# Two graph layers on 32 batches: place tables stored as rows, h scatters two steps apart, and the second regrouped batch's gathered tiles loaded later

## The chip, the core and the metric

The kernel runs on one core of a Trainium2 chip. The metric is the device time in microseconds (us) of one execution; lower is better. Before the change the median of three runs is 1025.54 us (1025.52 to 1026.99). The profile comes from one further execution, taken with the hardware profiler on.

## The reference

There are 32 batches of 512 nodes with 512 features. Two layers follow each other, each with a residual:

```python
h = jnp.maximum(_layernorm(x), 0.0)
x = x + (einsum('nm,bmd->bnd', adj, h) @ weight + bias)      # layer 0: graph aggregation
h = jnp.maximum(_layernorm(x), 0.0)
x = x + attention(h, adj)                                    # layer 1
# attention: 8 heads, scores + (1 - adj) * -1e9, softmax, @ v, @ Wo + bo
```

The adjacency matrix `adj` is sparse with weights between 0.05 and 1 (and ones on the diagonal, before scaling). In layer 1 the mask term is `(1 - adj) * -1e9`: a key whose weight is the largest of its row wins the softmax by a margin that no score can close. So the attention of a row is the value of a single node, the row's strongest neighbour.

## The kernel before, in words

**What is computed.** The kernel checks at run time that each row has a clear strongest neighbour; then layer 1 is a gather: `h` of the chosen rows goes through one combined matrix `wvo` (value times output projection), giving `z`, and each node adds the `z` row of its neighbour. Only rows that are somebody's strongest neighbour ("used", at most 336 of 512) need a `z`. Everything is float32, and the large products of 512x512 are done with a seven-product scheme (`product`, line 502): pieces "p1" to "c21", eight matmuls each.

**Two phases.** Batches 0 to 3 (`FIRST` = 4) run in a first phase with dense aggregation. Meanwhile the class `Plan` (line 974) works out a new order of the nodes, in which the adjacency matrix falls into blocks. A flag decides at a branch (lines 927 to 936), and the second phase, `sparse`, aggregates with fewer matmuls (`spread`, line 609). Batches up to 4 are held in natural order (`natural(b)`, line 458), later ones in the new order ("regrouped"). A regrouped batch's `x` rows are gathered from memory by `load_x`, and three extra 128-row tiles `plan.gx` (called `at` in the profile) by `load_g`; these are normalised into `plan.HG` (called `adjT`) before `spread`.

**The order of the work is written out by hand.** For every `b` there is a list of 21 steps (`todo`). `put(batch, step, f)` hangs a function on a step. Steps 0 to 6 go with the seven pieces of layer 0 of batch b, steps 7 to 13 with the aggregation of batch b+1 (in the sparse phase its four pieces take steps 7+8, 9+10, 11+12 and 13), steps 14 to 20 with the seven pieces of layer 1 of batch b-1. Each step's functions are issued after the matmuls of that piece and before the instruction that takes its result from PSUM. Each engine works through its own queue in this order. DMAs that POOL issues additionally wait for the last such result to be taken (`behind`, line 466).

**Round trips through memory around the change.**

- `put_h` (line 648) stores `h` of layer 1. For a natural batch it is four indirect scatters on POOL (line 661), one per 128 rows, to the places in `dest`, each followed by a small memset. For a regrouped batch it is four plain DMAs on SP (line 657).
- `get_h` (line 669) reads the used rows back with four DMAs on SP (line 672), after all four scatters of that batch have landed. `transpose_h` (line 723, VectorE) takes them in the next batch's steps 5, 7 and 8 (later in batch 1).
- `put_z` (line 734) stores `z` with DMAs on SP (line 741); `finish` (line 746) adds the `z` rows to `X` with four accumulating gathers on POOL (line 473); `store` writes the result.

**Place tables.** Three tables of 512 integers are written to memory and looked up with gathers of single elements:

- `table` from `dest` (`places`, line 579), made in batch 1 step 0 and looked up in steps 3 to 6;
- `posd` from `posi` (`save_pos`, line 1242), in batch 2 step 9, looked up in batch 5 (`look_1`);
- `tab2` from `pi` (`save_pi`, line 1248), in batch 6 step 4, looked up later in batch 6 (`look_2`).

In all three the source tile has node c*128+p in partition p, column c, and one DMA on SP stores it with the pattern "(c p) o -> p (c o)".

**Normalisation of the gathered tiles.** For batch 5 an object `lead` (`NormAct`: the statistics by ScalarE with accumulating activations, line 394, into a scrap tile) handles `gx` at the start of batch 4. For batch 6 and later a `NormMore` object (line 940) does it: `more_stats` (line 954) at steps 13 to 18 of the batch before the one that uses it, `more_relu` (line 967) at steps 1 to 3.

Of the kernel before, what the change touches and what calls it, by code (L numbers as in the profile page):

```python
# [8 lines left out]
F32 = mybir.dt.float32  # L9
I32 = mybir.dt.int32  # L10
# [8 lines left out]
P = 128  # L19
# [389 lines left out]
def single_path(ctx: ExitStack, tc: tile.TileContext, x, adj, out, kept, room):  # L409
    nc = tc.nc  # L410
    B, N, D = x.shape
# [10 lines left out]
    dram = ctx.enter_context(tc.tile_pool(name="dram", bufs=1, space=DRAM))  # L422
    dest = consts.tile([P, C], I32, name="dest")
    place = consts.tile([P, C], I32, name="place")
    pos = consts.tile([P, C], F32, name="pos")
# [29 lines left out]
    def run_phase(batches, sparse, small, ps_m, ps_t):  # L455
# [109 lines left out]
        def number_rows():  # L565
            counts = ps_t.tile([P, DC, P], F32, name="pt")
            nc.tensor.matmul(counts[:, 1, 0:C], upper, used, start=True, stop=True)
            nc.tensor.matmul(counts[:, 2, 0:1], upper, ones[:, 0:1], start=True, stop=True)
            nc.vector.tensor_add(pos, counts[:, 1, 0:C], before[:, 0:C])
            for m in range(C):  # L570
                nc.vector.tensor_scalar(other[:, m:m + 1], counts[:, 2, 0:1], float(m * P), before[:, C:C + 1],
                                        op0=ALU.add, op1=ALU.add)
            nc.vector.tensor_sub(other, other, pos)
            nc.vector.tensor_sub(pos, pos, other)
            nc.vector.tensor_mul(pos, pos, used)
            nc.vector.tensor_add(pos, pos, other)
            nc.vector.tensor_copy(dest, pos)

        def places():
            table = dram.tile([N, 1], I32, name="table", bufs=1)  # L580
            nc.sync.dma_start(table.rearrange("(c p) o -> p (c o)", p=P), dest)
            return table
# [93 lines left out]

        def get_all(b):
            for c in range(C):
                gather(hs[0][:, c, :], hs_d[b % 3], idx[:, c, 0:1] if natural(b) else plan.pq[:, c:c + 1])
# [69 lines left out]

        def fetch(b):  # L750
            for c in range(C):
                gather(late_z[b][:, c, :], z_d[b % 3], place_of(b, c))
# [22 lines left out]
        for b in batches:  # L775
            todo = [[] for _ in range(21)]

            def put(batch, step, f, *args):
                if 0 <= batch < B:
                    todo[step].append(lambda: f(batch, *args))  # L780

            if sparse and b == FIRST:
                for j in range(3):
                    put(b + 1, 1 + j, lambda b, j: lead.stats(j), j)
                put(b + 1, 3, lambda b: lead.power())
                put(b + 1, 4, lambda b: lead.offset())
                for j in range(3):
                    put(b + 1, 4 + (j + 1) // 2, lambda b, j: lead.relu(j), j)
            if sparse:
                for j, step in enumerate((6, 7, 8) if b == FIRST else (4, 5, 6)):  # L790
                    put(b + 2, step, load_g, [j])
                if last:
                    put(b + 1, 0, lambda b, n=last[-1]: n.offset())
                    for c in range(4):
                        put(b + 1, c, lambda b, c, n=last[-1]: n.relu(c), c)
                    for c in range(3):
                        put(b + 1, 1 + c, lambda b, c, n=last[-1]: n.more_relu(c), c)
# [5 lines left out]
            if b == B - 1:  # L803
                put(b - 2, 15, fetch)
            elif b < B:
                for c, step in enumerate((9, 11, 13, 15) if sparse and b == FIRST else (7, 9, 11, 13) if sparse else
                                         (4, 5, 6, 7) if ordered and b == FIRST - 1 else (1, 2, 3, 4)):
                    put(b - 2, step, finish, [c])
            elif not sparse:
                put(b - 2, 1, fetch)  # L810
# [30 lines left out]
            put(b, 10, lambda b: halves[0].relu(1, b < B - 1))  # L841
            put(b, 10, put_h, [0, 1] if sparse or b == B - 1 else [0])
            put(b, 11, lambda b: halves[1].relu(0, b < B - 1))
            if b < B - 1 and not sparse:
                put(b, 11, put_h, [1])
            put(b, 12, lambda b: halves[1].relu(1, b < B - 1))
            put(b, 12, put_h, [2, 3] if sparse or b == B - 1 else [2])
            if b < B - 1 and not sparse:
                put(b, 13, put_h, [3])
            if b < B - 1:  # L850
                if natural(b - 2):
                    put(b - 2, 19 if sparse and b == FIRST else 14 if sparse else 12, store)
                else:
                    for c in range(C):
                        put(b - 2, 14 + 2 * c, store, [c])
            if b < B - 1:
                put(b, 17, get_h)
            else:
# [10 lines left out]
            ahead = []  # L869
            kind = NormAct if on_act else NormMore if sparse else Norm  # L870
            if b == 0:
                put(2, 1, lambda b: ahead.append(ln0(b, kind)))
                for c, step in enumerate((1, 1, 2, 2)):
                    put(2, step, lambda b, c: ahead[0].stats(c), c)
            else:
                put(b + 2, 4 if sparse else 8, lambda b: ahead.append(ln0(b, kind)))
                for c, step in enumerate((9, 10, 13, 13)):
                    put(b + 2, step, lambda b, c: ahead[0].stats(c), c)
                if sparse:
                    put(b + 2, 4, lambda b: ahead[0].more(plan.gx, plan.HG, 3))  # L880
# [10 lines left out]
            if b == 0:  # L891
                put(0, 1, lambda b: number_rows())
                for i in (2, 3):
                    put(0, 8, lambda b, i: sum_b(nc, w0_t, w0_s, i), i)
                    put(0, 9, lambda b, i: sum_a(nc, wvo_t, wvo, i), i)
# [78 lines left out]
class Plan:  # L974
    def __init__(self, tc, consts, dram, adj, kept, upper, B):
# [5 lines left out]
        def t(name, shape, dt=F32):  # L981
            return consts.tile([P] + shape, dt, name=name)
# [22 lines left out]
        self.valid, self.gn, self.qn = t("valid", [3]), t("gn", [3]), t("qn", [C])  # L1005
        self.posi = t("posi", [C], I32)
        self.off = t("boff", [B, C])
        self.xi, self.gi = t("xi", [B, C], I32), t("gi", [B, 3], I32)
        self.pi, self.pq, self.place, self.pqf = t("pi", [C], I32), t("pq", [C], I32), t("pplace", [C], I32), t("pqf", [C])
        self.flag = consts.tile([1, 1], I32, name="flag2")  # L1010
# [242 lines left out]

    def packed(self):
        v = self.nc.vector
        v.tensor_copy(self.pqf, self.pq)
        v.tensor_copy(self.rank, self.pq)
# [3 lines left out]
        v.tensor_copy(self.place, self.pqf)  # L1261

# [22 lines left out]
    def schedule(self):  # L1285
        def at(b, step, f, *args):
            self.steps.setdefault(b, []).append((step, lambda ps_t, behind: f(*args)))
# [53 lines left out]
        at(7, 5, self.packed)  # L1341

# [260 lines left out]
```

## Time and profile before

| What | Value |
|---|---|
| median of 3 runs | 1025.54 us |
| profiled execution, its own time | 1038.36 us |
| span of the profiled execution | 1036.5 us |
| TensorE (PE) busy | 997.9 us, 96% |
| VectorE (DVE) busy | 800.1 us, 77% |
| ScalarE (ACT) busy | 585.8 us, 57% |
| GpSimd (POOL) busy | 589.1 us, 57% |
| DMA packets under 512 B | 17873 of 161140 |
| layer 0 of batches 3, 4 and 5 begins at | 153.25, 190.80, 229.16 us |

How to read it: all times count from the start of the span, in us. The slices are fortieths of the span (25.9 us each), a digit is the busy share in tenths. PEclk is the TensorE clock that was granted. A line of the wait view reads: engine, what waited, what ended the wait, and then the total in us, the number of waits and the longest. A line of the window view reads: stretch, its length, the busy time of PE, PEld (weight loads), DVE, ACT and POOL with their instruction counts, the granted clock, the mean busy share of the DMA engines (overlapping packets can bring it above 1) and the GB/s moved. A line of the timeline reads: start, duration, engine, line, operation, what is written from what, and in brackets the idle time before it and what ended it. "issue" means that no releaser is seen.

### The profile page before, as it was taken

How to read it: one execution, taken by the hardware profiler on the slowest of the kernel's cores; microseconds unless marked ns; L12 is line 12 of the kernel's file. 1: busy time of each engine (PE TensorE's matmuls, PEld its weight loads, DVE VectorE, ACT ScalarE, POOL GpSimd, SP SyncE). 2: the span in 40 equal slices, each digit the busy share in tenths (PEclk: the TensorE clock that was granted, in tenths of full speed). 3: DMA queues.
4: the chain of work that ended last, by engine and by line, in shares of the span. 5: the costliest groups of instructions: out<-in, count | busy, mean ns of one | idle time of the engine just before them, and what ended most of it. 6: DMA issues, size and time to landing. Idle time of an engine off the chain costs nothing. (4 is left out here: it accounts for less than half of the span.)

```text
span 1036.5 us, 17219 instructions
## 1 busy us (share of the span) xinstructions
PE 997.9 (96%) x5624; PEld 895.3 (86%) x5624; DVE 800.1 (77%) x1779; ACT 585.8 (57%) x1282; POOL 589.1 (57%) x666
## 2 busy tenths in 40 slices
PE   8999989889999999999999999999999999999984
PEld 7477878779999999999999999999999999999872
DVE  5996867668788777888877777788887777778761
ACT  3756353465555566665555556666555555666230
POOL 1033255556656666666666666666666666664436
PEclk9999989989999999999999999999999999999997
DMA  9316488777988888888788888888888888887664
GB/s 315 112 42 159 89 144 237 198 189 198 202 216 216 216 226 218 222 208 201 198 211 216 209 218 228 216 224 202 205 200 210 213 211 218 229 217 186 138 182 162
DMA packets 161140, 204.69 MB, mean 197 GB/s; under 512 B 17873, under 2 KB 105681, under 8 KB 161041
## 3 DMA queue, kind: packets, MB, share of 16 engines
q0 software_dynamic: 44544, 120.10, 48.1%
q1 hardware_dynamic: 115024, 81.99, 29.0%
q10 hardware_dynamic: 1472, 1.41, 0.4%
q8 instruction: 46, 0.75, 0.3%
q14 instruction: 54, 0.43, 0.1%
HBM read 121.45 MB, written 81.99 MB: 196 GB/s over the span
## 5 line engine op out<-in xcount | busy, mean ns | idle before, releaser
L562 DVE TENSOR_TENSOR x<-mm,x 128x512 f32<-128x512 f32 x217 | 148.9, 687 | 137.6 <-PE mm L506 111.0
L473 POOL DMA_INDIRECT x<-z,pplace x96 | 153.4, 1598 | 88.2 <-ACT yT L629 40.9
L379 ACT ACTIVATE h<-x,off,rstd 128x512 f32<-128x512 f32 x256 | 196.0, 804 | 6.2 <-DVE off L370 3.1
L506 PE MATMUL mm<-w_t,sel 128*128 128x256 f32 x744 | 172.4, 381 | 1.3 <-DVE x L562 1.2
L365 ACT ACTIVATE rstd<-mv,eps 128x2 f32<-128x2 f32 (+1 forms) x90 | 26.3, 292 | 245.4 <-DVE mv L362 241.1
L506 PEld LDWEIGHTS mm<-w_t,sel 128*128 128x128 f32 x744 | 141.3, 191 | 21.8 <-DVE x L562 2.4
L361 DVE BATCH_NORM_STATS2 st<-x 128x6 f32<-128x512 f32 x234 | 157.6, 674 | 1.1
L490 POOL DMA_INDIRECT out_dram<-x,xi x108 | 131.8, 1220 | 46.0 <-DVE zs L552 17.7
L621 PE MATMUL mm<-ap,h 128*128 128x256 f32 x648 | 157.7, 380 | 0.0
L473 POOL DMA_INDIRECT x<-in_x_dram,xi x108 | 104.0, 963 | 74.5 <-DVE x L562 26.9
L621 PEld LDWEIGHTS mm<-ap,h 128*128 128x128 f32 x648 | 114.9, 191 | 11.1
L506 PE MATMUL mm<-hTs,wvo_t 128*128 128x168 f32 x720 | 117.9, 314 | 6.1 <-ACT zs L554 5.6
L506 PE MATMUL mm<-w_s,yT 128*128 128x256 f32 x496 | 118.4, 382 | 3.1 <-ACT zs L554 3.1
L473 POOL DMA_INDIRECT at<-in_x_dram,gi x81 | 76.8, 948 | 71.9 <-DVE x L562 22.7
L506 PEld LDWEIGHTS mm<-hTs,wvo_t 128*128 128x128 f32 x720 | 109.2, 195 | 7.2 <-ACT zs L554 6.4
L554 ACT ACTIVATE zs<-mm,cvo_c 128x168 f32<-128x168 f32 x240 | 82.8, 398 | 43.4 <-PE mm L506 25.2
L506 PEld LDWEIGHTS mm<-w_s,yT 128*128 128x128 f32 x496 | 93.3, 191 | 14.9 <-ACT zs L554 3.4
L624 PEld LDWEIGHTS mm<-ag,adjT 128*128 128x128 f32 x648 | 89.3, 191 | 5.6
L624 PE MATMUL mm<-ag,adjT 128*128 128x128 f32 x648 | 89.7, 275 | 0.0
L596 DVE TENSOR_TENSOR x<-x,b_r 128x512 f32<-128x512 f32 x124 | 84.0, 678 | 0.0
L506 PE MATMUL mm<-hT,wvo 128*128 128x168 f32 x480 | 81.2, 314 | 0.0
L629 ACT COPY yT<-mm 128x512 f32<-128x512 f32 x108 | 61.6, 570 | 33.6 <-PE mm L624 29.2
(310 smaller groups left out, 1671.3 us busy)
## 6 DMA issues: line engine op xcount, KB each, us to landing
hc<-hs SPq DMA_DIRECT2D x124, 176.0 KB
z<-zr SPq DMA_DIRECT2D x120, 96.0 KB
hs<-h SPq DMA_DIRECT2D x52, 192.0 KB
z<-zr SPq DMA_DIRECT2D x120, 80.0 KB
hs<-h SPq DMA_DIRECT2D x52, 160.0 KB
out_dram<-x SPq DMA_DIRECT2D x20, 256.0 KB
x<-in_x_dram SPq DMA_DIRECT2D x12, 256.0 KB
x<-in_x_dram,xi POOLq DMA_INDIRECT x108
```

Of the source, the lines that this page charges most:

```text
L361: self.nc.vector.bn_stats(st, self.src[:, self.chunks[i], :])
L365: self.nc.scalar.activation(self.rstd[:, 0:len(self.chunks)], self.mv[:, :, 1], AF.Sqrt, bias=self.eps)
L379: self.nc.scalar.activation(dst, src, AF.Relu, bias=self.off[:, i:i + 1], scale=self.rstd[:, i:i + 1])
L473: return behind(nc.gpsimd.indirect_dma_start(out=dst, out_offset=None, in_=rows, in_offset=bass.IndirectOffsetOnAxis(ap=at, axis=0), **more))
L490: stored = behind(nc.gpsimd.indirect_dma_start(out=out_rows, out_offset=bass.IndirectOffsetOnAxis(ap=plan.xi[:, b, c:c + 1], axis=0), in_= ...
L506: nc.tensor.matmul(bank[:, m, 0:half], lhs[:, k, m * P:(m + 1) * P], rhs[:, k, :], start=(first and m == 0 and k == 0), stop=(k == 1), ski ...
L554: taken = nc.scalar.activation(dst[:, m, :], bank[:, m, :], AF.Identity, bias=cvo_c[:, 2 * i + m:2 * i + m + 1])
L562: return nc.vector.tensor_add(dst, bank, dst)
L596: nc.vector.tensor_add(X[b][:, c, :], X[b][:, c, :], b0_r)
L621: nc.tensor.matmul(two(bank, j), H0[b][:, j, cols], two(plan.ap[:, j, :], j), start=False, stop=False, skip_group_check=True)
L624: nc.tensor.matmul(bank[:, j * P:(j + 1) * P], extra[:, j - 1, cols], plan.ag[:, j - 1, j * P:(j + 1) * P], start=False, stop=(j == C - 1) ...
L629: tick(nc.scalar.copy(yT[:, d, :], bank))
```

## The change

Six things change.

1. **Tables as rows.** The places (float) are transposed by TensorE from 128x4 to 4x128, copied by VectorE to an integer tile of four partitions, and stored as four contiguous rows of 128. For `dest` this is `dest_rows` in batch 0 step 10; for `posd`, `row_pe` and `row_save` in batch 2 steps 10 and 11 (the store was in step 9); for `tab2`, a cast in batch 6 step 4, then steps 5 and 6 (the store was in step 4).
2. **h scatters of natural batches** go to steps 10, 12, 14 and 16. They were in 10, 11, 12 and 13 in batches 0 to 3, and in 10, 10, 12 and 12 in batch 4. `get_h` of these batches moves from step 17 to step 20.
3. **Table gathers in batch 3** (`tables`) go from steps 14 to 17 to steps 11, 13, 15 and 17.
4. **Gathered tiles of batch 6**: `load_g` for it moves from steps 6, 7, 8 to steps 15, 17, 19 of batch 4, and `lead` now normalises it too, at the start of batch 5, in place of `NormMore`. `load_g` for batch 7 moves from steps 4, 5, 6 to 6, 7, 8 of batch 5.
5. **finish**: in batch 4 from steps 9, 11, 13, 15 to 7, 9, 11, 13; in batch 5 the other way round.
6. **store**: in batch 4 from step 19 to 18, in batch 5 from 14 to 18.

`packed`, `fetch` and `get_all` get parameters without a change of what is issued.

```diff
+    dest_r = consts.tile([C, P], I32, name="dest_r")
...
+        def dest_rows():
+            pt = ps_t.tile([P, DC, P], F32, name="pt")
+            nc.tensor.transpose(pt[0:C, 0, :], pos, ident)
+            nc.vector.tensor_copy(dest_r, pt[0:C, 0, :])
+
         def places():
             table = dram.tile([N, 1], I32, name="table", bufs=1)
-            nc.sync.dma_start(table.rearrange("(c p) o -> p (c o)", p=P), dest)
+            nc.sync.dma_start(table.rearrange("(c p) o -> c (p o)", p=P), dest_r)
             return table
...
-            if sparse and b == FIRST:
+            if sparse and b <= FIRST + 1:
                 for j in range(3):
                     put(b + 1, 1 + j, lambda b, j: lead.stats(j), j)
                 put(b + 1, 3, lambda b: lead.power())
...
-                for j, step in enumerate((6, 7, 8) if b == FIRST else (4, 5, 6)):
+                for j, step in enumerate((15, 17, 19) if b == FIRST else (6, 7, 8) if b == FIRST + 1 else (4, 5, 6)):
                     put(b + 2, step, load_g, [j])
...
-                    for c in range(3):
+                    for c in range(3 if b > FIRST + 1 else 0):
                         put(b + 1, 1 + c, lambda b, c, n=last[-1]: n.more_relu(c), c)
...
-                for c, step in enumerate((9, 11, 13, 15) if sparse and b == FIRST else (7, 9, 11, 13) if sparse else
+                for c, step in enumerate((9, 11, 13, 15) if sparse and b == FIRST + 1 else (7, 9, 11, 13) if sparse else
                                          (4, 5, 6, 7) if ordered and b == FIRST - 1 else (1, 2, 3, 4)):
                     put(b - 2, step, finish, [c])
...
-            put(b, 10, put_h, [0, 1] if sparse or b == B - 1 else [0])
+            several = b == B - 1 or not natural(b)
+            put(b, 10, put_h, [0, 1] if several else [0])
             put(b, 11, lambda b: halves[1].relu(0, b < B - 1))
-            if b < B - 1 and not sparse:
-                put(b, 11, put_h, [1])
+            if not several:
+                for c in range(1, C):
+                    put(b, 10 + 2 * c, put_h, [c])
             put(b, 12, lambda b: halves[1].relu(1, b < B - 1))
-            put(b, 12, put_h, [2, 3] if sparse or b == B - 1 else [2])
-            if b < B - 1 and not sparse:
-                put(b, 13, put_h, [3])
+            if several:
+                put(b, 12, put_h, [2, 3])
             if b < B - 1:
                 if natural(b - 2):
-                    put(b - 2, 19 if sparse and b == FIRST else 14 if sparse else 12, store)
+                    put(b - 2, 18 if sparse and b <= FIRST + 1 else 14 if sparse else 12, store)
...
-                put(b, 17, get_h)
+                put(b, 20 if not several else 17, get_h)
...
-            kind = NormAct if on_act else NormMore if sparse else Norm
+            kind = NormAct if on_act else NormMore if sparse and b > FIRST else Norm
...
-                if sparse:
+                if kind is NormMore:
                     put(b + 2, 4, lambda b: ahead[0].more(plan.gx, plan.HG, 3))
...
+                put(0, 10, lambda b: dest_rows())
...
-        v.tensor_copy(self.posi, self.pos)
...
-    def save_pos(self):
-        self.nc.sync.dma_start(self.posd.rearrange("(c p) o -> p (c o)", p=P), self.posi)
+    def row_pe(self, ps_t, src):
+        self.ps_r = ps_t.tile([P, 4, P], F32, name="pt")
+        self.nc.tensor.transpose(self.ps_r[0:self.C, 0, :], src, self.kept["ident"])
+
+    def row_save(self, table):
+        self.nc.vector.tensor_copy(self.prow, self.ps_r[0:self.C, 0, :])
+        self.nc.sync.dma_start(table.rearrange("(c p) o -> c (p o)", p=P), self.prow)
...
-    def save_pi(self):
-        self.nc.sync.dma_start(self.tab2.rearrange("(c p) o -> p (c o)", p=P), self.pi)
+    def whole_pi(self):
+        self.nc.vector.tensor_copy(self.pqf, self.pi)
...
-        at(*divmod(k + 3, 21), self.save_pos)
+        pe(*divmod(k + 4, 21), self.row_pe, self.pos)
+        at(*divmod(k + 5, 21), self.row_save, self.posd)
...
-        move(3, (14, 15, 16, 17), self.tables)
+        move(3, (11, 13, 15, 17), self.tables)
...
-        at(6, 4, self.save_pi)
+        at(6, 4, self.whole_pi)
+        pe(6, 5, self.row_pe, self.pqf)
+        at(6, 6, self.row_save, self.tab2)
```

More of the change, by code (lines that the diff above doesn't have):

```diff
@@ L675, in get_h, with get_all @@
                         mybir.DependencyClass.Sync, mybir.DependencyReason.DATA), reason="all rows")
-        def get_all(b):
-            for c in range(C):
+        def get_all(b, chunks=range(C)):
+            for c in chunks:
                 gather(hs[0][:, c, :], hs_d[b % 3], idx[:, c, 0:1] if natural(b) else plan.pq[:, c:c + 1])
@@ L748, in finish, with fetch @@
                 gather(X[b][:, c, :], z_d[b % 3], place_of(b, c), compute_op=ALU.add)
-        def fetch(b):
-            for c in range(C):
+        def fetch(b, chunks=range(C)):
+            for c in chunks:
                 gather(late_z[b][:, c, :], z_d[b % 3], place_of(b, c))
@@ L856, in run_phase @@
             if b < B - 1:
-                put(b, 17, get_h)
-            else:
+                put(b, 20 if not several else 17, get_h)
+            elif b == B - 1:
                 put(b, 13, get_all)
@@ L1005, in __init__ @@
         self.valid, self.gn, self.qn = t("valid", [3]), t("gn", [3]), t("qn", [C])
-        self.posi = t("posi", [C], I32)
+        self.prow = consts.tile([C, P], I32, name="prow")
         self.off = t("boff", [B, C])
         self.xi, self.gi = t("xi", [B, C], I32), t("gi", [B, 3], I32)
-        self.pi, self.pq, self.place, self.pqf = t("pi", [C], I32), t("pq", [C], I32), t("pplace", [C], I32), t("pqf", [C])
+        self.pi, self.pq, self.place = (t(n, [C], I32) for n in ("pi", "pq", "pplace"))
+        self.pqf = t("pqf", [C])
         self.flag = consts.tile([1, 1], I32, name="flag2")
@@ L1240, in gather, with packed @@
                                                  in_offset=bass.IndirectOffsetOnAxis(ap=at, axis=0)))
-    def save_pos(self):
-        self.nc.sync.dma_start(self.posd.rearrange("(c p) o -> p (c o)", p=P), self.posi)
+    def row_pe(self, ps_t, src):
[4 more added lines that the diff above has]
+        self.nc.sync.dma_start(table.rearrange("(c p) o -> c (p o)", p=P), self.prow)
     def look_1(self, behind, c):
         self.gather(behind, self.pi[:, c:c + 1], self.posd, self.kept["idx"][:, c, 0:1])
-    def save_pi(self):
-        self.nc.sync.dma_start(self.tab2.rearrange("(c p) o -> p (c o)", p=P), self.pi)
+    def whole_pi(self):
+        self.nc.vector.tensor_copy(self.pqf, self.pi)
     def look_2(self, behind, c):
         self.gather(behind, self.pq[:, c:c + 1], self.tab2, self.xi[:, 0, c:c + 1])
-    def packed(self):
+    def packed(self, src, dst):
         v = self.nc.vector
-        v.tensor_copy(self.pqf, self.pq)
-        v.tensor_copy(self.rank, self.pq)
+        v.tensor_copy(self.pqf, src)
+        v.tensor_copy(self.rank, src)
         for lo, cut in ((128, 32), (256, 48), (384, 48)):
@@ L1260, in packed @@
             v.tensor_add(self.pqf, self.pqf, self.t1)
-        v.tensor_copy(self.place, self.pqf)
+        v.tensor_copy(dst, self.pqf)
     def rows(self, behind, c):
@@ L1338, in schedule @@
         move(5, (14, 16, 18, 20), self.look_1)
-        at(6, 4, self.save_pi)
+        at(6, 4, self.whole_pi)
+        pe(6, 5, self.row_pe, self.pqf)
+        at(6, 6, self.row_save, self.tab2)
         move(6, (14, 16, 18, 20), self.look_2)
-        at(7, 5, self.packed)
+        at(7, 5, self.packed, self.pq, self.place)
 @with_exitstack
```

## The prediction

> **What bounds the kernel now.** I read the page first, for its busy row, its slices and the clock.
>
> ```profile
> span 1036.5 us, 17219 instructions
> PE 997.9 (96%) x5624; PEld 895.3 (86%) x5624; DVE 800.1 (77%) x1779; ACT 585.8 (57%) x1282; POOL 589.1 (57%) x666
> ...
> PE   8999989889999999999999999999999999999984
> ...
> PEclk9999989989999999999999999999999999999997
> ```
>
> TensorE is the bound: from 234 us to 950 us it is never idle, so nothing that the change does to other engines there can shorten the run. What can be won lies in slices 5, 7 and 8 (and a little of 3), where both the PE row and the clock row dip. The waits of TensorE, longest first, say who ends the idle time:
>
> ```profile
> PE mm L506 <- ACT zs L554: 8.7, 4, 4.5
> PE pt L1224 <- issue: 3.7, 3, 1.9
> ...
> PE pt L1118 <- DVE u L1130: 2.1, 1, 2.1
> ```
>
> Placing these with the timeline gives four stalls. The window view of each (busy time of PE, PEld, DVE, ACT, POOL, then granted clock, DMA share, GB/s) gives its price:
>
> ```profile
> 96.00:108.00 12.00, 9.54 (x70) 9.03 (x69) 7.14 (x22) 5.17 (x16) 3.52 (x8) 0.86 0.47 149
> 132.00:152.00 20.00, 15.55 (x98) 14.66 (x97) 12.33 (x30) 11.01 (x26) 10.02 (x11) 0.83 0.87 136
> 186.00:196.00 10.00, 6.79 (x26) 5.46 (x25) 3.81 (x6) 4.83 (x13) 5.08 (x6) 0.83 1.01 266
> 212.00:228.00 16.00, 11.09 (x59) 10.34 (x58) 8.09 (x17) 8.71 (x24) 9.29 (x12) 0.79 0.85 192
> ```
>
> The loss is the idle time plus the clock not granted. A (batch 1): 2.46 + 0.14x12 = 4.1 us. B (batch 2): 4.45 + 0.17x20 = 7.9. C (the branch between the phases): 3.21 + 1.7 = 4.9. D (batch 4): 4.91 + 0.21x16 = 8.3. Together 25.2 us. The second terms agree with the Trainium skill, page "TensorE: Matmul & The Clock Gate", Part 1: an idle window of about 3.4 us halves the clock and a busy one restores it. By the wait list alone B would be worth 4.5 us; by the clock rows 7.9, which I take.
>
> **Part 1: tables as rows.** Each store of a place table (L581, L1243, L1249) writes 512 integers from 128 partitions, so 4 bytes at a time. Two-microsecond windows after the second of them, issued at 129.51:
>
> ```profile
> 130.00:132.00 2.00, 1.95 (x10) 1.40 (x9) 1.70 (x5) 2.00 (x5) 0.58 (x1) 1.00 1.50 203
> 132.00:134.00 2.00, 2.00 (x11) 1.77 (x10) 1.97 (x5) 1.97 (x6) 1.68 (x4) 1.00 2.78 29
> 134.00:136.00 2.00, 2.00 (x11) 1.77 (x10) 2.00 (x6) 1.97 (x5) 1.02 (x1) 1.00 1.00 14
> 136.00:138.00 2.00, 2.00 (x14) 1.92 (x14) 2.00 (x5) 1.62 (x6) 1.60 (x3) 1.00 0.31 7
> ...
> 140.00:142.00 2.00, 0.16 (x1) 0.19 (x2) 0.55 (x1) 0.00 (x0) 1.57 (x3) 1.00 1.09 399
> ```
>
> For 8 us the DMA engines move 7 to 29 GB/s with work waiting (the stores of a batch and four h scatters), then jump to 399. The same hole follows the table store at 79.05 (20 to 44 GB/s from 84 to 90) and the one at 265.48 (33 to 68 from 270 to 276). B begins inside the hole and ends when it does. The Trainium skill, page "DMA: Bandwidth & Descriptors", "Rules for kernel authors", says that a non-contiguous last dimension costs one descriptor per element. A sentence on the same page speaks against a gain: its fit in "Anatomy of one DMA", made for the Pool path, is 2.0 us plus bytes over 436 GB/s, so 2 KB would take an estimated 2.0 us whatever its shape, and rows would save nothing. The hole of 8 us decides: the shape counts here. A store of four 512-byte rows is in no trace; it costs between nothing and the same hole. I take nothing, because 512-byte packets are what the h and z stores are made of, and no hole follows those. So B goes: -7.9 (0 to -7.9). The holes at 79 and 265 cost TensorE nothing (it is 2.00 busy in each 2 us), but the first delays the place look-ups of batch 1 until 89.71, behind which the h scatters queue on POOL.
>
> Added for it: three transposes on TensorE's own queue, nearest row the 128x128 one at L1269, 273 ns: 3 x 0.27 = **+0.8 us** on the path (0 to 1). Three PSUM copies on VectorE (nearest L1283, 0.24 to 0.33 us) and a cast (0.13, against 0.17 saved at L1202) lie under matmuls; VectorE is 77% busy and has gaps of 0.4 to 1 us before the L562 adds. If it had none, they would cost 1 us. The new cast at batch 6 step 4 waits for the look-ups of batch 5; the SP queue, which waited for the same data before, issued at 265.48 without waiting, and step 4 is no earlier, so 0 (up to 1 us, with the add behind it on VectorE late next).
>
> **Part 2: h scatters two steps apart.** POOL's timeline:
>
> ```profile
> 94.76 1.15 POOL L661 DMA_INDIRECT hs<-h,dest  x1 [0.30 <-issue]
> ...
> 96.21 1.16 POOL L661 DMA_INDIRECT hs<-h,dest  x1 [0.19 <-issue]
> ...
> 97.67 0.96 POOL L661 DMA_INDIRECT hs<-h,dest  x1 [0.19 <-issue]
> ...
> 173.33 1.02 POOL L661 DMA_INDIRECT hs<-h,dest  x1 [4.28 <-ACT yT L544]
> ...
> 175.68 1.04 POOL L661 DMA_INDIRECT hs<-h,dest  x1 [1.20 <-DVE hTs L341]
> ...
> 211.51 1.01 POOL L661 DMA_INDIRECT hs<-h,dest  x1 [0.30 <-issue]
> ...
> 212.83 0.97 POOL L661 DMA_INDIRECT hs<-h,dest  x1 [0.19 <-issue]
> ```
>
> Batches 1 and 4 issue scatters 1.3 to 1.5 us apart, and both have a stall (A, D) in which ScalarE and VectorE stand with no engine named as releaser. Batch 3 issues the same four 1.7 to 2.4 us apart and has none; nor have the output scatters at 310 us and later, 1.8 us apart. After the change every pair has another POOL DMA or a whole step between: 2.5 us or more. So A and D go: -12.4 (0 to -12.4). Against it stands the same page, "Queues, rings and completion order": each DMA engine takes the queues in turn, packet by packet, so a burst on one queue should not starve another; by that rule spacing does nothing and A and D stay. The rows of batches 1, 3 and 4 decide for me, but they are three cases, so I keep 0 as an end.
>
> What is moved past what: the reload of h (L672) now waits for the scatter of step 16, not 13: about three pieces of layer 1, 3 x 1.14 = 3.4 us later, and the z stores follow it on SP. It ended at 148.14 before the transposes of 162.69 (batch 3), at 183.7 before 202.03, at 222.7 before 238.60. Allowing 3 us to land, 11 us remain, so it costs 0; each microsecond beyond would hold VectorE, then the adds, then TensorE. In batch 3 the four table gathers come between the scatters (steps 11 to 17): the first waits for the table written from 165.35 to 170, with a scatter behind it, perhaps 2 us, nobody's bound.
>
> **Part 3: batch 6's gathered tiles.** Their loads move from steps 6 to 8 to steps 15, 17 and 19 of batch 4; the adds of z come two steps sooner, and the stores of batch 2 (steps 19 to 18) no longer stand 5 us on SP for them. Six statistics of ScalarE (0.61 to 0.72 us each, with a read of 0.19) leave the stretch of stall D and go to steps 1 to 3 of batch 5, beside four activations: 4.5 + 3 x 0.72 + 0.3 = 7 us before the reciprocal on VectorE in step 4, which comes 7 to 8 us after the batch starts. It fits without a reserve. The last load is issued about 4 us before it is read; the three such loads before batch 4, issued from 186.37, were first read at 192.58, 6.2 us. So 0 to +2 us, taken as +0.5. In batch 5 the loads, adds and stores shift by two to four steps; POOL has 40% idle there.
>
> **The sum.** Against the profiled execution (1038.36 us, a span of 1036.5 and 1.9 around it): -7.9 - 12.4 + 0.8 + 0.5 = -19, so 1019 profiled. But the profiled execution is 12.8 us longer than the median of 1025.54, with the same matmuls; the excess can only be stalls. If all of it lies in A to D, the timed runs hold 25.2 - 12.8 = 12.4 us of them. Shared in proportion, A+B+D hold 10.0; if the branch C keeps its 4.9, they hold 7.5. Net -8.7 or -6.2. I take -7: **1018.5 us**, own range 1014 to 1022.5.
>
> **Rivals.** (1) *Only the hole goes*, the scatter stalls stay or move to other steps, as the queue rule has it: B's share 3.9 less 1.3, 1022.9. For it: ScalarE's idle time in D has no DMA as releaser. (2) *The stalls belong to profiling*: the timed runs have them elsewhere (the tail, the branch), and 1025.5 stays, give or take 2. For it: the 12.8 us. Against: a hole in the DMA service does not need a profiler. (3) *All of it*: the excess lies outside A to D and the timed runs gain up to 19: 1008. (4) *Slower*: the loads of batch 6 land late under the stores of batch 2 and the reload of h. ScalarE then stands in step 1 of batch 5 with batch 6's activations behind it, VectorE in step 4, and TensorE in layer 0. Price: latency less 4 us, plus 1.7 for the clock. It outweighs a gain of 7 from a latency of 9.5 us; at 14 us, 1018.5 + 11.7 - 0.5 = 1029.7. Against it: 6.2 us in a stretch of full DMA load.
>
> **Numbers.** Measurement tells about 0.2% (2 us) from no change. Forecast 0.56, (1) 0.14, (2) 0.15, (3) 0.07, (4) 0.08. Faster: 0.56 + 0.14 + 0.07 = 0.77; same 0.15; slower 0.08. The range reaches into (2) and leaves out (4) and most of (3): 1011 to 1027.
>
> **What would show it.** Right: no hole in GB/s after the three table stores; no TensorE wait at L1224; scatters 2.5 us apart and PE at 9 in slices 5 and 8; a wait only at the branch. Wrong: PE waits of 3 us or more at L506 in batches 1 to 5 with the clock at 0.5; ScalarE waiting on a DMA in step 1 of batch 5; or a profile as predicted with a median within 2 us of 1025.5, which would mean that the stalls were the profile's own.

## The result

The changed kernel takes 1021.1 us (median; 1018.62 to 1022.55) where the kernel before, measured beside it, takes 1025.53: a ratio of 0.9952, 95% interval 0.9933 to 0.9970, or 4 to 5 us less. Forecast was 1018.5.

From one comparison to the next the kernel before takes either 1022 to 1026 us (here the 1022 level) or 1037 to 1041 us (the 1040 level), and the other kernels move with it, so a ratio holds for the before that was timed beside it, and a profile is best set against one of the same level. The profile of before (1038.36) looks like one of the 1040 level, by its time and by a column that it lacks (last section); the profile of after that follows is of the 1022 level.

The page of after: span and busy time, the slices of TensorE and its clock.

```profile
span 1020.5 us, 17222 instructions
PE 989.0 (97%) x5627; PEld 888.4 (87%) x5627; DVE 800.5 (78%) x1783; ACT 586.0 (57%) x1282; POOL 590.8 (58%) x666
...
PE   8999999999999999999999999999999999999992
...
PEclk9999999999999999999999999999999999999997
```

The dips of the PE row in slices 5, 7 and 8 are gone. The waits of TensorE in after:

```profile
PE pt L126 <- DMA x<-in_L_gnn_Wv_dram: 3.3, 2, 2.0
PE mm L507 <- ACT zs L555: 2.8, 2, 2.1
```

The wait at L1224 is gone, and the one for ScalarE's evacuation of PSUM (L554 before, L555 now) fell from 8.7 to 2.8 us. The windows in which stalls A to D lay, and the one behind them (busy PE, PEld, DVE, ACT, POOL, then granted clock, DMA share, GB/s):

```profile
96.00:108.00 12.00, 12.00 (x108) 11.39 (x107) 11.41 (x30) 9.80 (x24) 3.92 (x7) 1.00 0.28 106
132.00:152.00 20.00, 20.00 (x137) 18.41 (x136) 18.02 (x38) 10.05 (x24) 14.89 (x15) 1.00 0.64 192
...
186.00:196.00 10.00, 9.56 (x49) 8.23 (x49) 7.00 (x18) 6.36 (x14) 4.94 (x5) 1.00 0.75 258
212.00:228.00 16.00, 16.00 (x87) 14.22 (x86) 8.16 (x17) 9.68 (x21) 6.00 (x7) 1.00 0.78 217
228.00:240.00 12.00, 9.83 (x55) 9.20 (x55) 10.40 (x27) 9.27 (x24) 9.75 (x9) 0.86 0.82 175
```

A, B and D read 0 here. In the last window there is a stall that before does not have, call it E: 2.17 us idle and 0.14x12 = 1.7 of clock, 3.9 us. After the second table store, issued at 131.29, the DMA engines go on moving data:

```profile
132.00:134.00 2.00, 2.00 (x11) 1.77 (x10) 2.00 (x6) 1.97 (x5) 0.56 (x1) 1.00 0.72 263
134.00:136.00 2.00, 2.00 (x14) 1.90 (x13) 2.00 (x5) 1.97 (x7) 1.49 (x3) 1.00 0.78 299
```

That is 263 and 299 GB/s where before moved 29 and 14 in the same windows. Stall E can be followed back through the timeline of after (start, duration, engine, line, and in brackets the idle time before and its releaser):

```profile
208.82 0.98 POOL L667 DMA_INDIRECT hs<-h,dest  x1 [0.30 <-issue]
...
213.79 1.85 SPq L678 DMA_DIRECT2D hc<-hs  x4
...
222.71 0.71 DVE L729 STREAM_TRANSPOSE hT<-hc 128x512 f32<-128x512 f32 x1 [3.12 <-DMA z<-zr]
```

The last scatter of batch 4 is issued at 208.82, the reload of h follows at 213.79, and VectorE's transpose of that tile stands until 222.71. The profile names z<-zr as releaser, but the operand is hc; two other profiles of the changed kernel (those with sixteen more stores, below) name the reload itself, the first of them so:

```profile
220.66 0.71 DVE L729 STREAM_TRANSPOSE hT<-hc 128x512 f32<-128x512 f32 x1 [3.53 <-DMA hc<-hs]
```

From issue to use that is 9 us, at a mean DMA share of 1.0 from 216 to 224 us, with the z stores on the same engines. The delay is then handed on: VectorE's statistics of batch 6 come late, ScalarE's activations behind them too, and ScalarE takes a piece of layer 1 at 234.34, 2.8 us after its matmuls end; TensorE waits for that until 235.08.

### The profile page after: what moved, and what is told of

Read it like the earlier page. It is cut to its first block, busy times and chain, and to the rows that moved or that the text cites. A ratio compares the mean times of both kernels' runs of the same rounds, so it can differ in the third digit from the quotient of the medians.

```text
span 1020.5 us, 17222 instructions
## 1 busy us (share of the span) xinstructions
PE 989.0 (97%) x5627; PEld 888.4 (87%) x5627; DVE 800.5 (78%) x1783; ACT 586.0 (57%) x1282; POOL 590.8 (58%) x666
## 5 line engine op out<-in xcount | busy, mean ns | idle before, releaser
L507 PE MATMUL mm<-hTs,wvo_t 128*128 128x168 f32 x720 | 114.7, 309 | 2.2 <-ACT zs L555 2.1
L507 PEld LDWEIGHTS mm<-hTs,wvo_t 128*128 128x128 f32 x720 | 106.5, 192 | 3.0 <-ACT zs L555 2.7
L555 ACT ACTIVATE zs<-mm,cvo_c 128x168 f32<-128x168 f32 x240 | 83.1, 399 | 39.7 <-PE mm L507 39.2
L507 PE MATMUL mm<-hT,wvo 128*128 128x168 f32 x480 | 78.8, 307 | 0.0
```

The costliest lines, as they stand in the source:

```text
L507: nc.tensor.matmul(bank[:, m, 0:half], lhs[:, k, m * P:(m + 1) * P], rhs[:, k, :], start=(first and m == 0 and k == 0), stop=(k == 1), ski ...
L555: taken = nc.scalar.activation(dst[:, m, :], bank[:, m, :], AF.Identity, bias=cvo_c[:, 2 * i + m:2 * i + m + 1])
```

## The experiments

To compare kernels I read the loss of TensorE (idle time, plus the clock not granted times the window) in four stretches of the profile: 92 to 124 us (batch 1, stall A), 124 to 160 (batch 2, B), 160 to 200 (batch 3 and the branch, C), 200 to 245 (batches 4 and 5, D and E). For the kernel before of the first profile they are 4.1, 7.7, 4.8 and 8.5.

**Rows alone.** The kernel before with part 1 and nothing else. As a diff against after, this takes back among others

```
-                for c in range(1, C):
-                    put(b, 10 + 2 * c, put_h, [c])
+                put(b, 11, put_h, [1])
...
-                put(b, 20 if not several else 17, get_h)
+                put(b, 17, get_h)
```

> The kernel before with part 1 alone: the three tables go out as rows, every step of the scatters, reloads and gathers stays. Theory T (the holes in the DMA service are real in every execution, and spaced scatters do the rest): no hole after the three stores, stall B is gone from the profile (profiled about 1030 us against 1038), and the timed median falls by 3 to 4 us, to about 1022. Rival Q (the stalls belong to profiling): the profile falls by about 8 us as well, but the timed median stays within 1 us of before. Rival S (spacing the scatters is the whole gain): stall B shrinks to the price of a burst of scatters, the median stays at before, and A and D are as they were.

Measured at the 1022 level: 1014.96 us, ratio 0.9923 (0.9896 to 0.9951). Losses 0.0, 0.0, 0.8, 0.0; the two stretches of stalls B and D:

```profile
124.00:160.00 36.00, 36.00 (x218) 32.21 (x218) 31.00 (x76) 19.78 (x45) 22.34 (x21) 1.00 0.66 189
...
200.00:245.00 45.00, 45.00 (x257) 41.51 (x256) 34.84 (x71) 27.90 (x61) 28.57 (x29) 1.00 0.90 238
```

And the scatters of batch 4, as close as before (1.3 to 3.2 us apart), with TensorE never idle behind them:

```profile
195.03 1.01 POOL L667 DMA_INDIRECT hs<-h,dest  x1 [0.30 <-ACT yT L635]
196.34 0.98 POOL L667 DMA_INDIRECT hs<-h,dest  x1 [0.19 <-issue]
199.52 1.18 POOL L667 DMA_INDIRECT hs<-h,dest  x1 [0.30 <-issue]
201.00 1.47 POOL L667 DMA_INDIRECT hs<-h,dest  x1 [0.19 <-ACT zs L555]
```

So at this level the rows alone gain 7.2 us, twice what was expected of them and as much as was forecast for the whole change, and close scatters by themselves stop nothing.

**Parts 2 and 3 alone.** The changed kernel with its tables as columns again:

```
-            nc.sync.dma_start(table.rearrange("(c p) o -> c (p o)", p=P), dest_r)
+            nc.sync.dma_start(table.rearrange("(c p) o -> p (c o)", p=P), dest)
```

and the same for the other two.

> The changed kernel with part 1 undone: the tables are stored by columns again, 4 bytes at a time, the rest as changed. Theory T: the hole after the store of batch 2 is back and TensorE stands in it; profiled about 1030, median 3 to 4 us above the changed kernel (about 1024.5). Rival Q: the hole and a stall are back in the profile, the median stays at the changed kernel's 1021. Rival S: the median stays at 1021, and the profile shows a hole but no stall, since the scatters no longer come in a burst on top of it.

Measured in the same comparison: 1025.57, ratio 1.0024 (1.0006 to 1.0042): slower. Losses 0.0, 3.8, 3.8, 2.3. Stall B is there, and so is the hole, in two-microsecond windows:

```profile
130.00:132.00 2.00, 2.00 (x11) 1.75 (x10) 2.00 (x5) 1.97 (x5) 0.63 (x1) 1.00 1.04 8
132.00:134.00 2.00, 2.00 (x14) 1.90 (x13) 2.00 (x5) 1.97 (x7) 1.41 (x3) 1.00 0.60 8
134.00:136.00 2.00, 1.73 (x28) 1.59 (x27) 2.00 (x4) 0.47 (x1) 1.26 (x1) 1.00 0.46 24
136.00:138.00 2.00, 0.65 (x9) 0.51 (x9) 0.89 (x2) 0.43 (x2) 1.84 (x2) 1.00 0.99 351
```

That is 8 GB/s with 104% and 60% of the engines' time taken; the stall starts at its end. With scatters two steps apart the hole is as deep as before, so it comes with the store's shape.

**Sixteen stores more.** The changed kernel with a 2 KB table store in every batch from 10 to 25, once in columns and once in rows, to a table that nobody reads:

```
+    def save_extra(self):
+        self.nc.sync.dma_start(self.extra.rearrange("(c p) o -> p (c o)", p=P), self.pi)
...
+        for b in range(10, 26):
+            at(b, 9, self.save_extra)
```

> The changed kernel with 16 more stores of a table by columns into a scratch table, one in each of batches 10 to 25 at step 9; nothing reads it. This prices one hole in the steady part. If a hole stops TensorE by itself, as in B (7.9 us in the profile, 3 to 4 us by my share in timed runs), the median rises by 50 to 60 us and the profile by over 100. If a hole only delays what is in flight and the schedule has room for it, as the hole at 267 us had, TensorE stays at 100% and the median rises by 0 to 10 us. Rival Q: profile far up, median unchanged.

> The same 16 stores to a scratch table, as rows of 128 (four packets of 512 bytes each). All theories: no holes, median within 1 us of the changed kernel's 1021, as a store of 2 KB takes 0.3 us of SP's queue. If it rises as in the run with columns, the price is that of one more DMA on SP's queue and not of its packets.

Measured in the same comparison: columns 1020.61, ratio 0.9984 (0.9965 to 1.0004); rows 1020.06, ratio 0.9980 (0.9962 to 0.9998). The columns leave a hole behind the store issued at 390.37:

```profile
392.00:394.00 2.00, 2.00 (x11) 1.77 (x10) 0.96 (x2) 0.00 (x0) 0.72 (x2) 1.00 1.04 286
394.00:396.00 2.00, 2.00 (x11) 1.77 (x10) 1.58 (x3) 0.00 (x0) 1.22 (x2) 1.00 1.54 113
396.00:398.00 2.00, 2.00 (x12) 1.77 (x12) 1.90 (x6) 0.15 (x1) 1.01 (x2) 1.00 0.36 43
398.00:400.00 2.00, 2.00 (x15) 1.87 (x14) 1.97 (x5) 0.73 (x2) 1.34 (x1) 1.00 0.41 37
```

and the sixteen land in 10.3 to 11.3 us; behind the rows the same windows read 308, 172, 162 and 137 GB/s. TensorE is busy 699.45 of the 700 us from 260 to 960 with columns, 699.44 with rows. So sixteen holes cost nothing here. That a hole is paid for only where something behind it is waited for is my reading of this and of stall B; no run moves a store step by step.

The changed kernel itself was not run in this comparison. The nearest to it is the one with rows: 1020.06, against 1014.96 of rows alone, and its profile loses 5.4 us in the four stretches against 0.8. So parts 2 and 3 seem to cost some 5 us on top of the rows at this level. Against its own before, though, the changed kernel measured 0.9952, and that interval overlaps the one of rows alone (0.9896 to 0.9951).

**Leaving out part 2 or part 3.** Parts 1 and 3 (scatters close, reload at step 17; first lines), and parts 1 and 2 (loads of batch 6 at steps 6 to 8 of batch 4, with their statistics, z adds and stores in their old steps; last lines):

```
-                    put(b, 10 + 2 * c, put_h, [c])
+                put(b, 11, put_h, [1])
...
-        move(3, (11, 13, 15, 17), self.tables)
+        move(3, (14, 15, 16, 17), self.tables)
...
-                for j, step in enumerate((15, 17, 19) if b == FIRST else (6, 7, 8) if b == FIRST + 1 else (4, 5, 6)):
+                for j, step in enumerate((6, 7, 8) if b == FIRST else (4, 5, 6)):
```

> Parts 1 and 3 without part 2: the h scatters stand close again, the reload of h comes at step 17, the tables at steps 14 to 17. Theory (the late reload of h, a consequence of the spacing, makes the stall of 233 to 235 us in batch 5): no such stall, the reload of batch 4 lands before 219 us, and the time is that of rows alone, 0.992 of before (1014 to 1017). Rival 1 (the loads and statistics of part 3 make it): the stall stays, 0.995 (1020 to 1022). Rival 2 (the two together, either alone fits): no stall in batch 5, 0.992. The prediction on record says of this kernel that the stalls of batches 1 and 4 come back with the close scatters: 8 to 12 us more in the profiled execution than after, about 1021 to 1025 timed.

> Parts 1 and 2 without part 3: the loads of batch 6's gathered tiles and their statistics are where they were before. Theory (late reload): the stall in batch 5 stays in some form, since the reload is as late as in after, 0.995 (1019 to 1022). Rival 1 (part 3): no stall of over 1 us in batch 5, 0.992 (1014 to 1017). Rival 2 (the two together): 0.992 too, with the reload landing late and VectorE waiting for it all the same.

This comparison is of the 1040 level (before 1039.46). Parts 1 and 3: 1025.07, ratio 0.9863 (0.9843 to 0.9882), losses 0.7, 0.0, 3.9, 5.5. Parts 1 and 2: 1027.52, ratio 0.9876 (0.9855 to 0.9897), losses 0.1, 0.4, 9.1, 4.3. The two can't be told apart in time, and stall E shows in neither, so they don't decide whether part 2 or part 3 makes it. But their profiles say more than their times. Without part 3, D is there in spite of the spacing: TensorE waits 2.54 us for ScalarE at 208.5 to 211.0. With part 3 and close scatters D is not there; the 5.5 is another stall, in layer 0 of batch 5:

```profile
217.53 0.63 ACT L394 ACTIVATE ph<-at 128x512 bf16<-128x512 f32 x1 [5.29 <-DMA at<-in_x_dram,gi]
...
223.79 0.18 DVE L404 RECIPROCAL rstd<-rstd 128x3 f32<-128x3 f32 x1 [5.43 <-ACT rstd L401]
...
224.81 1.65 PE L507 MATMUL mm<-w_t,yT 128*128 128x256 f32 x3 [3.73 <-DVE x L563]
```

ScalarE stands for the first gathered tile of batch 6, issued at 209.73 beside the reload of h; VectorE stands for the statistics, and TensorE for the add behind them. That is rival 4 of the prediction, step by step.

**One table as rows; spacing alone.** The kernel before with the second table alone as rows (first lines), and with part 2 alone (last lines):

```
-        at(*divmod(k + 3, 21), self.save_pos)
+        pe(*divmod(k + 4, 21), self.row_pe, self.pos)
+        at(*divmod(k + 5, 21), self.row_save, self.posd)
...
+                for c in range(1, C):
+                    put(b, 10 + 2 * c, put_h, [c])
...
-                put(b, 17, get_h)
+                put(b, 20 if not several else 17, get_h)
```

> The kernel before with one table alone, the second (batch 2), stored as rows; the first and the third stay columns and the scatters stay close. The prediction's account: the stall of batch 2 goes (7.9 us in the profiled execution), those of batches 1 (4.1) and 4 (8.3) stay, and a third of the gain of the rows shows in the time: 0.997. Rival (the later stalls follow from the delay of batch 2): the stall of batch 4 goes as well, that of batch 1 stays, 0.994 or less. Second rival (the first table matters most): nothing over 0.2%.

> The kernel before with part 2 alone: scatters two steps apart, reload of h at step 20, tables between; the tables stay columns and part 3 is left out. The prediction's account: stalls of batches 1 and 4 go, that of batch 2 stays, 12 us less in the profiled execution and 0.995 to 0.997 timed. Theory now (spacing is worth nothing or less): within 0.2% of before, or slower by up to 0.4%, whatever the profiled execution shows, with the hole of 7 to 30 GB/s after the second table in place.

Same comparison. The second table alone: 1030.9, ratio 0.9913 (0.9894 to 0.9932), losses 2.4, 0.0, 2.2, 7.5. Stall B goes, A and D stay: the first expectation holds for the profile. The time falls by 8.6 us, as much as B costs in a profile of this level and three times the 0.3% expected. Spacing alone: 1034.69, ratio 0.9961 (0.9944 to 0.9978), losses 1.0, 5.4, 3.5, 4.3: A mostly gone, D halved, B left. Spacing is worth 0.4% here, against a loss of 0.2% at the other level for parts 2 and 3 together.

**Before, after and rows side by side.** No edit but that of rows alone.

> The kernel before, unchanged, profiled and timed beside the next two on one chip; the medians of before were 1022 us on one chip and 1039 us on another. Theory (the length of the stalls differs from chip to chip): its profiled execution lies within 5 us of its own median on the same chip, with the stalls A to D in the profile as long as that time asks for: about 25 us in all where the time is 1038, 8 to 12 us where it is 1022. Rival, on record in the prediction (the stalls belong to profiling): the profiled execution is 10 us or more over the median on the same chip.

> The changed kernel beside rows alone on the same chip. Theory (rows are the whole gain, parts 2 and 3 cost 3 us): 0.995 of before on a chip where before takes 1022 to 1026 us, with the stall of batch 5; on a chip where before takes 1036 to 1040, where each part gained on its own, 0.985 to 0.988. Rival (on the chip with long stalls spacing and rows add up): 0.983 or less there.

> Rows alone again (the kernel before with part 1). Theory: faster than the changed kernel by 0.2 to 0.5% on whichever chip; on a chip with long stalls 0.981 to 0.985 of before. Rival (rows alone leave the burst stalls A or D on a chip with long stalls, and spacing is worth its reload there): slower than the changed kernel by 0.2% or more there, with a stall of batch 1 or 4 in the profile.

Again the 1040 level: before 1041.11 (run as a kernel of its own 1039.47, ratio 0.9991). After: 1025.73, ratio 0.9846 (0.9821 to 0.9870). Rows alone: 1028.7, ratio 0.9863 (0.9835 to 0.9891). The stretches of before, profiled at 1039.32 us:

```profile
92.00:124.00 32.00, 29.16 (x202) 25.15 (x201) 24.29 (x62) 13.36 (x32) 10.76 (x15) 1.00 0.45 125
124.00:160.00 36.00, 31.16 (x187) 27.87 (x186) 26.38 (x68) 19.08 (x47) 17.84 (x18) 0.91 0.92 161
160.00:200.00 40.00, 37.37 (x192) 33.14 (x192) 26.79 (x57) 18.73 (x41) 23.28 (x26) 0.96 0.85 225
200.00:245.00 45.00, 39.47 (x218) 36.17 (x217) 31.30 (x69) 21.33 (x46) 26.11 (x28) 0.92 0.72 185
```

of after, at 1027.71:

```profile
92.00:124.00 32.00, 32.00 (x231) 28.59 (x230) 27.43 (x74) 17.62 (x44) 11.30 (x13) 1.00 0.41 99
124.00:160.00 36.00, 35.27 (x214) 31.39 (x213) 30.65 (x75) 18.42 (x43) 18.62 (x19) 1.00 0.62 184
160.00:200.00 40.00, 36.10 (x182) 31.85 (x181) 26.24 (x58) 19.41 (x41) 24.54 (x27) 0.96 0.82 220
200.00:245.00 45.00, 43.27 (x265) 40.39 (x264) 36.59 (x86) 30.08 (x70) 30.19 (x31) 1.00 0.83 199
```

and the last two of rows alone, at 1030.62:

```profile
160.00:200.00 40.00, 35.81 (x182) 31.83 (x181) 26.22 (x58) 19.40 (x41) 23.04 (x27) 0.96 0.80 220
200.00:245.00 45.00, 39.71 (x224) 36.92 (x223) 31.45 (x72) 24.65 (x53) 26.35 (x28) 0.92 0.75 191
```

Losses: before 2.8, 8.1, 4.2, 9.1; after 0.0, 0.7, 5.5, 1.7; rows alone 0.5, 0.0, 5.8, 8.9. The profiled before agrees with its own median, so the stalls don't need a profiler. After and rows alone have intervals that overlap, so the expectation that rows alone are the faster is not borne out here. And D, which rows alone did not have at the 1022 level, is there in full at this one, and absent in after (its 1.7 is one wait for an add of VectorE at 222.00, in batch 5). The scatters of rows alone stand as close as at the other level (203.66, 204.97, 208.15, 209.44). In D of before (about 214 to 221 us of this profile) ScalarE's queue shows what is in the way:

```profile
218.77 0.63 ACT L954 ACTIVATE adjT<-at 128x512 f32<-128x512 f32 x1 [2.38 <-DMA hs<-h,dest]
...
219.48 0.58 ACT L629 COPY yT<-mm 128x512 f32<-128x512 f32 x1
219.96 0.70 ACT L554 ACTIVATE zs<-mm,cvo_c 128x168 f32<-128x168 f32 x2
```

The first line is the statistics of batch 6, which part 3 moves away, and the profile names a scatter of h for its wait. The copy behind it on the same queue is what VectorE waits for (6.05 us), the evacuation what TensorE waits for (4.51 us).

**Batch 4 alone close.** The changed kernel with

```
-                    put(b, 10 + 2 * c, put_h, [c])
+                    put(b, 10 + (c if b == FIRST else 2 * c), put_h, [c])
```

> The changed kernel with the h scatters of batch 4 alone close again (steps 10 to 13); tables as rows, batches 0 to 3 spaced, reload of h at step 20, gathered loads later. Theory (close scatters make the stall of batch 4, on the chips with long stalls): where before takes 1036 to 1041, batch 4 (200 to 245 us of the profile) loses 5 to 9 us of TensorE against 1.7 in after, batches 1 and 2 lose under 1, and the time is 0.988 to 0.991 of before, against 0.985 of after. Where before takes 1022 to 1026: no stall there from the scatters, the reload of h lands before 219 us, the stall of batch 5 goes, 0.992 to 0.994. Rival (the spacing of batch 4 has no part in it): the same losses as after, 0.985 on a chip of the first kind and 0.995 on one of the second.

Measured with before at 1036.84: 1026.97, ratio 0.9903 (0.9878 to 0.9928), losses 0.0, 0.0, 5.7, 1.6. The time is the theory's, the profile the rival's: no stall D. The profiled execution (1022.61) is the quickest of its six, 4.4 us under their median, and in it the edit made only one pair of scatters close (203.18 and 204.50; the others have gathers between them). So by itself it decides little on the spacing.

All profiles of the 1040 level together, by TensorE's idle time in D (us):

| Scatters of batch 4 | without part 3 | with part 3 |
|---|---|---|
| close | 4.9, 5.5 (before), 3.9 (second table), 5.3 (rows alone) | none (parts 1 and 3; batch 4 close) |
| spaced | 2.5 (spacing alone), 2.5 (parts 1 and 2) | none (after) |

Spacing halves D; part 3 removes it, with close scatters too. At the 1022 level no profile has D, with or without part 3.

## Why the prediction was right, and where it was wrong

- **B and the hole: right.** Every profile with the second table as rows loses 0.0 to 0.9 us in batch 2; every one with columns loses 3.8 to 8.1. The size forecast (7.9 in the profile) fits the matched pair, 8.1 to 0.7. The fit of the Trainium skill, page "DMA: Bandwidth & Descriptors", section "Anatomy of one DMA", which is made for the Pool path and by which 2 KB would take an estimated 2.0 us whatever their shape, does not hold for these stores on SP's queue: the sixteen column stores landed in 10.3 to 11.3 us. That rows would leave no hole, taken by analogy with the h and z stores, held. So did "the holes at 79 and 265 cost TensorE nothing", in the form of sixteen more of them.
- **A and D by spacing: half right for A, luck for D.** "So A and D go: -12.4". In the matched pair at the 1040 level they do go (2.8 to 0.0, 9.1 to 1.7). But A goes with the rows alone too (0.5 and 0.0), as it mostly does with spacing alone (1.0); it seems to need a late look-up and a burst together. D goes by part 3: spacing leaves 2.5 us of idle time, part 3 leaves none with either spacing. The text saw that six statistics of ScalarE "leave the stretch of stall D" and gave that no gain. It also read ScalarE and VectorE in D as standing "with no engine named as releaser"; the wait view of before names one, the statistics of batch 6:

```profile
DVE sel L329 <- ACT adjT L954: 4.4, 1, 4.4
```

  By the rule weighed there (the Trainium skill, "DMA: Bandwidth & Descriptors", "Queues, rings and completion order": the queues are served in turn) spacing does nothing. At the 1022 level no run speaks against that; at 1040 the halved D does. In time the spacing is not seen on top of the rows.
- **"It costs 0": the step that failed.** The reload of h was given 11 us of slack. (By the text's own figures the tightest case is 162.69 - 148.14 - 3.4 - 3 = 8.1.) For batch 4 the slack was read from a trace in which stall D holds up TensorE while the reload goes on: its issue ended at 222.7 and the first use came at 238.60, 15.9 us later. In rows alone at the 1022 level, without D and with the reload where it was, 7.1 us are left:

```profile
204.36 2.93 SPq L678 DMA_DIRECT2D hc<-hs  x4
...
214.37 0.70 DVE L729 STREAM_TRANSPOSE hT<-hc 128x512 f32<-128x512 f32 x1
```

  In after it is issued 4.5 us behind the start of batch 5's layer 0 (209.30), in rows alone 0.6 us ahead of it (204.93): 5.1 us later and not 3.4, and 9 us pass from issue to use. The wait that the text named ("each microsecond beyond would hold VectorE, then the adds, then TensorE") is what happened: stall E, 3.9 us. That the reload makes E is read from its chain and not shown by a run that moves the reload alone; a wait of 1.5 us for part 3's statistics (forecast to fit "without a reserve") lies just ahead of it, at 218.63, and its share is open.
- **C keeps its 4.9: open.** At the 1022 level the branch lost 1.2 in after; at 1040 it lost 5.5, no less than the 4.2 of before. The two levels differ there more than the kernels do, and no run takes the branch apart.
- **The sum.** -19 was forecast for the profiled execution. The matched pair gives 1039.32 to 1027.71, -11.6, although the losses fell by 24.2 - 7.9 = 16.3. Idle time fell by 9.6 (43.2 to 33.6) and TensorE's busy time by 2.2 only, where the granted clock of the windows said 6.8. The formula counts some time twice: a low clock costs nothing while TensorE stands. In D of before, from 218 to 220 us, the window reads 0.00 us busy at a clock of 0.70, so these 2 us are in the loss as 2.6. That may not be the whole difference; the four stretches of my comparison are read by the same formula and are too high in the same way. Two slips bear on nothing: the gain of rival 3 would give 1006.5 and not 1008, and rival 4 breaks even at 9.8 us by its own sum, not 9.5.
- **Profile to timed: a number near the mark, for another reason.** The text took the 12.8 us between profiled execution and median as stalls, scaled A to D down to 12.4 and came to -7; measured is -4.4. By all signs that execution was one of the 1040 level, while the timed runs were of the 1022 level, where no profile of any kernel shows D (before itself was not profiled there). Rival 2, "the stalls belong to profiling", falls with the 1039.32 beside 1039.47. That the -4.4 is the rows' own gain (7.2 us at the 1022 level) less stall E fits the numbers; that it came near -7 is luck.
- **Rival 4** (batch 6's loads land late) did not come in after, where ScalarE waits 1.39 us for them; it came in parts 1 and 3, where their first tile takes 7.8 us from issue to use, beside the reload of h. So early reloads seem to make these loads late, and late reloads make stall E.

At the 1022 level parts 2 and 3 without the rows are slower than before by 0.2%, and rows alone has the lowest time; at 1040 it can't be told from the whole change.

## What to carry to other kernels

Write a small table that will be looked up by address as long rows, even at the price of a transpose on the busiest engine: it is the only part here that gained at both levels. Before paying for it, ask what waits behind the store, since sixteen such stores in the steady part cost nothing. Slack that is read from a trace with a stall goes when the stall goes. When a load is moved later, take its landing time from the trace in the stretch into which it goes, not from its size, and follow its first reader. And where a change has several parts, test which of them ends which stall.

## What was not expected of the hardware

- One kernel has two levels of time, about 1.5% apart, which did not mix within a comparison: before took 1022.15 (59 runs, none over 1029.02) and 1036.84 (11 runs, none under 1034.1) under the same chip number at different times. Of the 17.8 us between the two profiles of rows alone (1012.8 and 1030.6), 14.4 lie in the losses of 92 to 245 us (0.8 against 15.2). The records differ too. The landings of POOL's gathers from 260 to 960 us, in the DMA view of rows alone at the 1022 level, have a last column (median us to landing):

```profile
x<-z,pplace POOLq DMA_INDIRECT x96, 5.6
out_dram<-x,xi POOLq DMA_INDIRECT x96, 5.0
```

and at the 1040 level the column is empty:

```profile
x<-z,pplace POOLq DMA_INDIRECT x94
x<-in_x_dram,xi POOLq DMA_INDIRECT x92
```

  In every profile of the 1040 level it is empty, that of before included, and in every one of the 1022 level it is filled. What sets the level isn't known; no run here tries it. Without these records a wait for such a DMA may be put down to another engine at the 1040 level.
- What starts D at the 1040 level stays open. In rows alone, 203 to 214 us, ScalarE's copy at 208.98 has stood 3.1 us and the profile names TensorE, but the matmuls that it copies ended at 205.7; VectorE then stands 4.6 us and TensorE 4.5 us for ScalarE. So the wait that comes first is for something that the profile doesn't name.
